# Second pass of a state-space layer: normalise before the last projection, with its weights held still

## The chip, the cores and the metric

The kernel runs on one core of one Trainium2 chip. The metric is device time in microseconds (us) of one execution, lower is better; the median of three runs is quoted. A core has these engines: PE (TensorE: matrix products and transposes from SBUF into PSUM, with weight loads shown apart as PEld), DVE (VectorE), ACT (ScalarE), POOL (GpSimd) and SP, which here issues the DMA transfers. Everything is in fp32, where one logical product is two PE instructions.

## The reference

The input x is 4 images of 64 channels and 256 x 256 pixels. Layer 0 adds a gated convolution with a spectral part to x; the change doesn't touch it. Layer 1 normalises its input by groups and runs two state-space blocks over the pixels, one along the rows (d = 0) and one along the columns (d = 1), and fuses them:

```
def s5_block(x, d):                  # x: tokens x 64 channels
    fx = layer_norm(x, ln1)          # over the channels
    h  = scan(fx)                    # forward and backward linear recurrence, + D * fx
    z  = gelu(h) + fx
    f2 = layer_norm(z, ln2)
    return f2 @ enc.T @ dec.T + f2
x = x + fusion_w @ concat(s5_block(rows, 0), s5_block(columns, 1)) + fusion_b
```

The part that matters is the last: the mean and variance of z over the 64 channels of each token, the scaling by 1 / sqrt(var + eps), and a 64 x 64 map per direction. The kernel folds the centring, the gain, enc, dec, the identity and the fusion into one matrix W of each direction (block `NB[d]` of the table `wb[d]`, the same 64 x 64 block twice on the diagonal). What is left at run time is the factor r = (var + eps)^-0.5 of each token, and the product with W.

## The kernel before, in words

Layer 0 leaves its result in `x1d` in DRAM. Layer 1 then goes over each of the 4 images in turn: pass A (`pass_a`) normalises, stores fx as `fxd` and sums up the states of short stretches; `scan` runs the recurrences over these summaries; pass B (`pass_b`), the one that is changed, works through the image again in 16 strips of 16 rows, each as two units: a column unit (d = 1), then a row unit (d = 0). So there are 32 units an image and 128 in all. The 128 partitions are 2 x 64 channels: their two halves are two sets of rows of the strip.

A unit holds 2048 columns of 128 partitions, in four blocks of 512, taken in the order `blocks = (1, 2, 0, 3)`. Its steps are:

- `load`: the unit's fx (1 MB) by one DMA, two units ahead, into one of three buffers.
- `states`: products of fx into the PSUM tile `pst` (one buffer of two banks), and for each half of it a DVE operation that advances the state (state x step + product), into `stm` or `sto`. A row unit does this in 8 parts of two steps, a column unit in 4 parts of one or two.
- `filt`: the products that make h of a block in PSUM (`ph`), then GELU on ACT, the addition of fx on POOL (together z, the tile `xr`), and the square `sq` on ACT.
- `sums`: products with a constant that give the sum of squares and the sum over 64 channels, for four blocks in one PSUM tile (`pv`), and a copy of it to SBUF on ACT.
- `rstd_of`: four transposes, four small DVE operations, and the power on POOL, so r lies with tokens on the partitions.
- `outputs`, for each block: four 128x128 products with z as the weights and W moving, which gives W z with tokens on the partitions (`px`), and one DVE multiplication with r (`y`).
- `emit`, for each block: four transposes of `y` back to channels on the partitions, and one DVE addition onto the strip's sum `acc`; for the row unit also the bias, and after the last block the four stores to the output.

The loop of pass B pipelines this over units. Iteration n has four quarters, i = 0 to 3, each of two parts. In quarter i it runs `filt` of unit n for one block, `states` of the next unit (in quarter 0 the last group of unit n itself), and late steps of units n - 1 and n - 2, by the table `behind`, whose key (4k + i, part) stands for the unit n - k. Before the change each quarter has an `outputs` and an `emit`; `sums` stands at (4, 1), `rstd_of` at (5, 1).

The order of instructions on PE and DVE is that of the program: products go through `mm`, DVE operations through the helper `vec`, and both are held in program order. ACT, POOL and SP instructions of pass B aren't held; the compiler places them by its own estimate of when they are ready. PSUM has eight banks: `pst` two, `ph` two, `pv` one, `px` three. In the profile, L1351 is `mm` of pass B, L303 the helper of DVE, L1469 the transposes in `rstd_of`, L1493 those in `emit`, L1445 GELU, L1446 POOL's addition, L1447 the square, L1460 the copy of the sums, L1476 the power, L1371 and L1377 the copies of carried states, L207 `mm` of layer 0.

Of the kernel before, what the change touches and what calls it, by code (L numbers as in the profile page):

```python
# [12 lines left out]
ALU = mybir.AluOpType  # L13
# [3 lines left out]
C = 64  # L17
HID = 170
S = 256
P = 128  # L20
# [8 lines left out]
NS0 = S // R0  # L29
R1 = 16  # L30
# [6 lines left out]
def _layout(parts):  # L37
# [8 lines left out]
    [("ident", 128), ("swap", 128), ("nswap", 128), ("cen", 128), ("gm", 128), ("on2", 34), ("sgn", 1), ("qf", 64),  # L46
# [12 lines left out]
def _constants():  # L59

    out = np.zeros((P, CONST_N), np.float64)

    def put(name, a):
        o, w = CONST_AT[name]
        out[: a.shape[0], o : o + w] = a

    eye = np.eye(P)
    swap = np.roll(eye, C, axis=0)
    put("ident", eye)
    put("swap", swap)  # L70
# [4 lines left out]
    put("on2", np.kron(np.eye(2, 34, 2), np.full((C, 1), 1.0 / C)))  # L75
    put("sgn", np.concatenate([-np.ones((C, 1)), np.ones((C, 1))]))
# [34 lines left out]
def tile_kernel(ctx: ExitStack, tc: tile.TileContext, x, cst, w0, winp, wdwp, w1, out):  # L111
    nc = tc.nc
# [17 lines left out]
    ident, swap, nswap = con("ident"), con("swap"), con("nswap")  # L130
# [63 lines left out]
    with ExitStack() as l0:  # L194
# [70 lines left out]
        stats1 = new(gpool, [P, 2 * NS0, 6], "stats0", 1)  # L265
# [12 lines left out]
        with ExitStack() as l1w:  # L278
            sp = l1w.enter_context(tc.tile_pool(name="prep1", bufs=1))
            lw = l1w.enter_context(tc.tile_pool(name="ldw", bufs=8))  # L280
# [796 lines left out]

    norms = new(gpool, [P, nb, 2], "norms", 1)
# [172 lines left out]
    def scan(tabs):  # L1251
        with ExitStack() as es:
# [8 lines left out]
            nc.vector.tensor_tensor(fold[:, 0], ident[:, 0:C], swap[:, 0:C], ALU.add)  # L1261
# [52 lines left out]
    def pass_b(b):  # L1314

        with ExitStack() as es:
# [6 lines left out]
            def load(s, d):  # L1323
                fx = new(ld, [P, 8 * S], "fx", 3)
                nc.sync.dma_start(out=fx, in_=fxd[b][s, d])
                return fx

            order = [(s, d) for s in range(NS1) for d in (1, 0)]
            units = []

            def unit(n):
                s, d = order[n]
                units.append({"s": s, "d": d, "fx": load(s, d)})

            nc.sync.dma_start(out=wb[1].rearrange("p a b -> p (a b)"), in_=wdb[1])
            unit(0)
            nc.sync.dma_start(out=wb[0].rearrange("p a b -> p (a b)"), in_=wdb[0])
            unit(1)
            accs = {0: load_strip(b, 0)}
# [17 lines left out]
            STEPS = (16, 8)  # L1357
# [21 lines left out]
            def states(u, i, part):  # L1379
# [5 lines left out]
                if d == 1:  # L1385
                    fx = u["fx"].rearrange("p (r w) -> p r w", r=8)
                    js = [j for j in (2 * i - 1, 2 * i) if j >= 0]
                    for n, j in enumerate(js):
                        mm(ps[:, n], lhsT=wb[1][:, j], rhs=fx[:, both(j, 7)], start=True, stop=True)
# [5 lines left out]
                fx = u["fx"].rearrange("p (q t) -> p q t", q=16)  # L1395
                js = (4 * i + 2 * part, 4 * i + 2 * part + 1)
                for n, j in enumerate(js):
                    for h in range(2):
                        p = slice(h * C, (h + 1) * C)
                        mm(  # L1400
                            ps[:, h, n * 256 : (n + 1) * 256], lhsT=wb[0][p, j], rhs=fx[p, both(j, 15)], start=True, stop=True
                        )
# [7 lines left out]
            def filt(u, i, part):  # L1410

                d, w = u["d"], wb[u["d"]]
                fx = u["fx"][:, i * 512 : (i + 1) * 512]
# [28 lines left out]
                xr, sq = new(wk, [P, 512], "xr", 8), new(wk, [P, 512], "sq", 4)  # L1442
# [7 lines left out]
            def sums(u):  # L1450

                ps = new(pp, [P, 512], "pv", 1)
                for k, name in enumerate(("sq", "xr")):
                    for i in range(4):
                        mm(
                            ps[32 * i : 32 * i + 32], lhsT=con("on2")[:, 2 - 2 * k : 34 - 2 * k], rhs=u[name, i], start=(k == 0),
                            stop=(k == 1),
                        )
                u["sums"] = new(wk, [P, 512], "sums", 1)
                nc.scalar.copy(u["sums"], ps)  # L1460
                for i in range(4):
                    u.pop(("sq", i))

            def rstd_of(u):

                ps = new(pp, [P, 512], "pv", 1)
                t = u.pop("sums")
                for k in range(4):
                    tc.keep_in_program_order(nc.tensor.transpose(ps[:, k * P : (k + 1) * P], t[:, k * P : (k + 1) * P], ident))  # L1469
                m = new(wk, [P, 16, 4], "m4")  # L1470
                vec.tensor_copy(m, ps.rearrange("p (n c) -> p n c", c=32)[:, :, 0:4])
                ve, r = new(wk, [P, 16, 2], "ve"), new(wk, [P, 32], "rs")
# [3 lines left out]
                nc.gpsimd.tensor_tensor(r, ve.rearrange("p n c -> p (n c)"), mhalf, ALU.pow)  # L1476
                u["r"] = r.rearrange("p (k i h) -> p k i h", k=4, i=4)

            def outputs(u, i):


                ps, xr = new(pp, [P, 512], "px", 3), u.pop(("xr", i))
                for k in range(4):
                    mm(ps[:, k * P : (k + 1) * P], lhsT=xr[:, k * P : (k + 1) * P], rhs=wb[u["d"]][:, NB[u["d"]]], start=True, stop=True)
                y = u["y", i] = new(wk, [P, 512], "y")
                yv, pv = (t.rearrange("p (k h c) -> p k h c", k=4, h=2) for t in (y, ps))
                vec.tensor_tensor(yv, pv, u["r"][:, :, i].unsqueeze(3).to_broadcast([P, 4, 2, C]), ALU.mult)

            def emit(u, i):
                y, acc = u.pop(("y", i)), u["acc"]  # L1490
                ps = new(pp, [P, 512], "px", 3)
                for k in range(4):
                    tc.keep_in_program_order(nc.tensor.transpose(ps[:, k * P : (k + 1) * P], y[:, k * P : (k + 1) * P], ident))  # L1493
                if u["d"] == 1:
                    o = acc[:, 2 * i : 2 * i + 2].rearrange("p r (g q) -> p r q g", q=16)
                    vec.tensor_tensor(o, ps.rearrange("p (r q g) -> p r q g", r=2, q=16), o, ALU.add)
                    return
                o = acc.rearrange("p r (g q) -> p q (r g)", q=16)[:, 4 * i : 4 * i + 4]
                vec.scalar_tensor_tensor(o, ps.rearrange("p (q t) -> p q t", q=4), bias, o, ALU.add, ALU.add)
                if i == blocks[-1]:  # L1500
                    for h, r, row in rows_of(u["s"]):
                        nc.sync.dma_start(out=out[b, :, row : row + 7 : 2, :], in_=acc[h, r])
# [4 lines left out]
            behind = {}  # L1507
            for i, k in enumerate(blocks):
                behind[7 + i, 1] = [(outputs, k)]
                behind[8 + i, 0] = [(emit, k)]  # L1510
            behind[4, 1] = [(sums,)]
            behind[5, 1] = [(rstd_of,)]

# [4 lines left out]
            for n in range(len(order) + 3):  # L1518
                if n < len(order):
                    s, d = order[n]  # L1520
                    units[n]["acc"] = accs[s]
                    if n + 2 < len(order):
                        unit(n + 2)
                    if d == 0 and s + 1 < NS1:
                        accs[s + 1] = load_strip(b, s + 1)
                    elif d == 0 and b + 1 < nb:
                        accs[NS1] = load_strip(b + 1, 0)
                for i in range(4):
                    m, group = (n, 3) if i == 0 else (n + 1, i - 1)

# [100 lines left out]
```

## Time and profile before

| | us |
|---|---|
| median of three runs (8789.25 to 8792.47) | 8791.17 |
| profiled execution: its span, first to last instruction (the profile gives no other time of it) | 8795.4 |
| PE busy in it | 8386.9 (95%) |
| DVE busy | 7055.1 (80%) |
| ACT busy | 3411.4 (39%) |
| POOL busy | 2401.9 (27%) |

The span of the profiled execution is 4.2 us above the median. A busy time is the union of an engine's instructions; matmuls are pipelined, so they overlap, and the distance between the starts of two steps says more than the length of one. Shapes are written as rows*columns of the weights, then the moving operand: `64*128 64x256` has weights of 64 rows and 128 columns, and 256 moving columns. A group of instructions is given with its count, busy time, mean duration in ns and the idle time before it with what ended that.

### The profile page before, as it was taken

How to read it: one execution, taken by the hardware profiler on the slowest of the kernel's cores; microseconds unless marked ns; L12 is line 12 of the kernel's file. 1: busy time of each engine (PE TensorE's matmuls, PEld its weight loads, DVE VectorE, ACT ScalarE, POOL GpSimd, SP SyncE). 2: the span in 40 equal slices, each digit the busy share in tenths (PEclk: the TensorE clock that was granted, in tenths of full speed). 3: DMA queues.
4: the chain of work that ended last, by engine and by line, in shares of the span. 5: the costliest groups of instructions: out<-in, count | busy, mean ns of one | idle time of the engine just before them, and what ended most of it. 6: DMA issues, size and time to landing. Idle time of an engine off the chain costs nothing. (4 is left out here: it accounts for less than half of the span.)

```text
span 8795.4 us, 184922 instructions
## 1 busy us (share of the span) xinstructions
PE 8386.9 (95%) x79478; PEld 5721.3 (65%) x79478; DVE 7055.1 (80%) x8837; ACT 3411.4 (39%) x5158; POOL 2401.9 (27%) x1282
## 2 busy tenths in 40 slices
PE   3999999999999999998999989999989999899999
PEld 2666666666666666665566657566655666565666
DVE  6999999999999999996767657776757677576766
ACT  3444444444444444445522237222264222462222
POOL 3000000000000000003734446544456444474444
PEclk9999999999999999999999999999999999999999
DMA  7444344444444333334423336133263233452332
GB/s 174 106 102 103 98 103 101 104 102 98 103 104 101 87 88 84 84 80 142 151 68 82 91 90 214 59 80 89 73 183 116 80 82 80 123 196 53 82 89 65
DMA packets 655264, 904.19 MB, mean 103 GB/s; under 512 B 43120, under 2 KB 584816, under 8 KB 618864
## 3 DMA queue, kind: packets, MB, share of 16 engines
q1 hardware_dynamic: 654448, 892.37, 37.9%
q8 instruction: 627, 10.27, 0.5%
q14 instruction: 189, 1.55, 0.1%
HBM read 583.86 MB, written 275.05 MB: 98 GB/s over the span
## 5 line engine op out<-in xcount | busy, mean ns | idle before, releaser
L207 PE MATMUL m<-v,sw 64*128 64x256 f32 (+1 forms) x8192 | 1542.8, 393 | 1.5 <-DVE v L303 1.1
L207 PEld LDWEIGHTS m<-v,sw 64*128 64x128 f32 (+1 forms) x8192 | 1123.4, 188 | 504.0 <-issue 359.0
L303 DVE SCALAR_TENSOR_TENSOR acc<-xat,taps,acc 128x1024 f32<-128x1024 f32 x1024 | 1311.0, 1280 | 16.6 <-ACT acc L164 2.9
L1446 POOL TENSOR_TENSOR xr<-xr,fx 128x512 f32<-128x512 f32 x512 | 650.3, 1270 | 1862.3 <-ACT xr L1445 1367.7
L1351 PE MATMUL pst<-fx,wb 64*128 64x256 f32 (+1 forms) x4992 | 1016.1, 438 | 37.5 <-DVE stm L303 18.3
L694 POOL MEMSET at<- 64x256 f32 x4 | 1.2, 308 | 3526.2 <-DVE v L303 3526.2
L1351 PEld LDWEIGHTS pst<-fx,wb 64*128 64x128 f32 (+1 forms) x4992 | 508.8, 187 | 370.4 <-issue 244.1
L1476 POOL TENSOR_TENSOR rs<-ve,mhalf 128x32 f32<-128x32 f32 x128 | 695.3, 5432 | 99.5 <-DVE ve L303 99.5
L303 DVE SCALAR_TENSOR_TENSOR stm<-stm,step,pst 128x512 f32<-128x512 f32 x640 | 478.5, 748 | 232.9 <-PE pst L1351 219.4
L1447 ACT ACTIVATE sq<-xr 128x512 f32<-128x512 f32 x512 | 322.9, 631 | 873.7 <-POOL xr L1446 873.7
L207 PEld LDWEIGHTS m<-ct,hw 128*64 128x64 f32 x16384 | 509.8, 138 | 117.6 <-issue 117.6
L303 DVE SCALAR_TENSOR_TENSOR sto<-sto,step,pst 128x512 f32<-128x512 f32 x512 | 382.9, 748 | 242.4 <-PE pst L1351 231.1
L1351 PE MATMUL px<-wb,xr 128*128 128x128 f32 x4096 | 574.1, 284 | 0.0
L1351 PEld LDWEIGHTS px<-wb,xr 128*128 128x128 f32 x4096 | 524.2, 194 | 54.0 <-issue 41.8
L303 DVE TENSOR_TENSOR y<-px,rs 128x512 f32<-128x512 f32 x512 | 354.0, 691 | 230.6 <-PE px L1351 221.6
L1351 PE MATMUL ph<-sto,wb 128*64 128x128 f32 (+1 forms) x5120 | 528.1, 299 | 0.0
L207 PE MATMUL m<-ct,hw 128*64 128x64 f32 x16384 | 527.4, 223 | 0.0
L1351 PE MATMUL ph<-stm,wb 128*64 128x128 f32 (+1 forms) x5120 | 525.1, 299 | 0.0
L1351 PEld LDWEIGHTS ph<-stm,wb 128*64 128x64 f32 (+1 forms) x5120 | 409.3, 147 | 144.2 <-issue 127.9
L1351 PEld LDWEIGHTS ph<-sto,wb 128*64 128x64 f32 (+1 forms) x5120 | 405.3, 147 | 142.7 <-issue 129.6
L1445 ACT ACTIVATE xr<-ph 128x512 f32<-128x512 f32 x256 | 152.8, 597 | 825.9 <-PE ph L1351 825.9
L164 POOL TENSOR_TENSOR rs<-ve,mhalf 128x32 f32<-128x32 f32 x64 | 347.6, 5432 | 398.5 <-DVE ve L303 386.8
(317 smaller groups left out, 15636.0 us busy)
## 6 DMA issues: line engine op xcount, KB each, us to landing
strip<-x1d SPq DMA_DIRECT2D x512, 256.0 KB, 7.3
fx<-fxd SPq DMA_DIRECT2D x128, 1024.0 KB, 6.9
at<-in_x_dram SPq DMA_DIRECT2D x248, 320.0 KB, 4.6
sx<-in_x_dram SPq DMA_DIRECT2D x256, 256.0 KB, 4.0
pr<-in_x_dram SPq DMA_DIRECT2D x256, 256.0 KB, 4.1
er<-in_x_dram SPq DMA_DIRECT2D x256, 256.0 KB, 4.0
x1d<-x SPq DMA_DIRECT2D x256, 256.0 KB, 3.9
fxd<-fv SPq DMA_DIRECT2D x64, 1024.0 KB, 4.7
```

The source lines that it names most:

```text
L164: return lambda *args, **kw: tc.keep_in_program_order(getattr(self.engine, name)(*args, **kw))
L207: tc.keep_in_program_order(nc.tensor.matmul(*args, **kw))
L303: tc.keep_in_program_order(getattr(nc.vector, name)(*args, **kw))
L694: nc.gpsimd.memset(at[C:P, 4, 1 : S + 1], 0.0)
L1351: tc.keep_in_program_order(nc.tensor.matmul(*args, **kw))
L1445: nc.scalar.activation(xr, ps if d == 1 else xr, AF.Gelu_apprx_tanh)
L1446: nc.gpsimd.tensor_tensor(xr, xr, fx, ALU.add)
L1447: nc.scalar.activation(sq, xr, AF.Square)
L1476: nc.gpsimd.tensor_tensor(r, ve.rearrange("p n c -> p (n c)"), mhalf, ALU.pow)
```

## The change

The order of the last two operations is turned round: z is multiplied by r first, with channels on the partitions, and then projected with W as the weights and z moving, so the result comes out with channels on the partitions.

- `rstd_of` writes the power into a tile `wide`, cleared once per image, at two of each 32 columns.
- `rows_back` (new): four transposes of `wide`, and an ACT copy into `rows`: the factors of block i lie as rows 32i and 32i + 1.
- `scale` (new), twice per unit, for a pair of blocks: two products of 32 rows, with the constant `pick` as weights, spread the factors over the 64 channels of each half in two banks of PSUM; one DVE multiplication of 128x1024 scales z in place.
- `project` (new), twice per unit: four products with 64x64 weights (one block of W each), 512 moving columns, into two banks; then one DVE addition of 128x1024 onto the sum. The products read z in the order of the output, so the moving operand steps by 16 elements (column unit) or 128 elements (row unit).
- `outputs` and `emit` are gone. The table of late steps becomes: `sums` (4, 1), `rstd_of` (5, 1), `rows_back` (7, 1), `scale` (8, 0) and (8, 1), `project` (9, 0) and (9, 1). The stores come with the second `project` of a row unit.
- The strip's sum lies differently on the partitions (`load_sum`, `rows_at`): halves by the upper and lower eight rows.
- fx is loaded in two halves, outer blocks (0, 3) and inner blocks (1, 2), the inner one in quarter 2 and into two buffers; z is kept in pairs of blocks.
- PSUM: `pst` two banks, `ph` two, and a tile `two` of two banks, twice, for all late steps. Constant `swap` is gone and `pick` added; `stats1` moves to another pool; some buffers go from two to one.

```diff
-            def load(s, d):
-                fx = new(ld, [P, 8 * S], "fx", 3)
-                nc.sync.dma_start(out=fx, in_=fxd[b][s, d])
-                return fx
+            def load(u, inner):
+                t = u["fx", inner] = new(ld, [P, 1024], f"fx{inner}", 2 if inner else 3)
+                v = fxd[b][u["s"], u["d"]]
+                if inner:
+                    nc.sync.dma_start(out=t, in_=v[:, 512:1536])
+                else:
+                    nc.sync.dma_start(
+                        out=t.rearrange("p (k c) -> p k c", k=2),
+                        in_=v.rearrange("p (k c) -> p k c", k=4)[:, 0:4:3],
+                    )
...
-                nc.gpsimd.tensor_tensor(r, ve.rearrange("p n c -> p (n c)"), mhalf, ALU.pow)
-                u["r"] = r.rearrange("p (k i h) -> p k i h", k=4, i=4)
-
-            def outputs(u, i):
-                ps, xr = new(pp, [P, 512], "px", 3), u.pop(("xr", i))
-                for k in range(4):
-                    mm(ps[:, k * P : (k + 1) * P], lhsT=xr[:, k * P : (k + 1) * P], rhs=wb[u["d"]][:, NB[u["d"]]], start=True, stop=True)
-                y = u["y", i] = new(wk, [P, 512], "y")
-                yv, pv = (t.rearrange("p (k h c) -> p k h c", k=4, h=2) for t in (y, ps))
-                vec.tensor_tensor(yv, pv, u["r"][:, :, i].unsqueeze(3).to_broadcast([P, 4, 2, C]), ALU.mult)
-
-            def emit(u, i):
...
+                nc.gpsimd.tensor_tensor(
+                    wide.rearrange("p k (i c) -> p (k i) c", c=32)[:, :, 0:2], ve,
+                    mhalf.rearrange("p (n c) -> p n c", c=2), ALU.pow,
+                )
+
+            def rows_back(u):
+                ps = new(pp, [P, 2, 512], "two")[:, 0]
+                turn_blocks(ps, lambda k: wide[:, k])
+                u["rows"] = new(wk, [P, 512], "rows", 1)
+                nc.scalar.copy(u["rows"], ps)
+
+            def scale(u, n):
+                k = u["first"][n]
+                ps, x = new(pp, [P, 2, 512], "two"), u["pairs"][k]
+                for place, i in enumerate((k, 2 + k) if u["d"] == 1 else (2 * k, 2 * k + 1)):
+                    p = slice(32 * i, 32 * i + 32)
+                    mm(ps[:, place], lhsT=con("pick")[p], rhs=u["rows"][p], start=True, stop=True)
+                vec.tensor_tensor(x, x, ps, ALU.mult)
+
+            def project(u, n):
+                d, k = u["d"], u["first"][n]
+                x, ps = u["pairs"].pop(k), new(pp, [P, 2, 512], "two")
+                for hi in range(2):
+                    for h in range(2):
+                        p = slice(h * C, (h + 1) * C)
+                        if d == 1:
+                            v = x[p, hi].rearrange("p (r q g) -> p r g q", r=2, q=16)
+                        else:
+                            v = x[p].rearrange("p b (q r g) -> p r g (b q)", q=4, r=8)[:, 4 * hi : 4 * hi + 4]
+                        mm(ps[hi * C : (hi + 1) * C, h], lhsT=wb[d][p, NB[d], p], rhs=v, start=True, stop=True)
+                if d == 1:
+                    o = u["acc"][:, :, 2 * k : 2 * k + 2].rearrange("p k r w -> p k (r w)")
+                    vec.tensor_tensor(o, ps, o, ALU.add)
+                    return
+                o = u["acc"].rearrange("p k r (g q) -> p (k r) g q", q=16)[:, :, :, 8 * k : 8 * k + 8]
+                vec.scalar_tensor_tensor(
+                    o, ps.rearrange("p k (r g q) -> p (k r) g q", r=4, g=16), bias, o, ALU.add, ALU.add
+                )
...
             blocks = (1, 2, 0, 3)
-            behind = {}
-            for i, k in enumerate(blocks):
-                behind[7 + i, 1] = [(outputs, k)]
-                behind[8 + i, 0] = [(emit, k)]
-            behind[4, 1] = [(sums,)]
-            behind[5, 1] = [(rstd_of,)]
+            behind = {
+                (4, 1): [(sums,)], (5, 1): [(rstd_of,)], (7, 1): [(rows_back,)], (8, 0): [(scale, 0)],
+                (8, 1): [(scale, 1)], (9, 0): [(project, 0)], (9, 1): [(project, 1)],
+            }
...
+                    if i == 2 and n + 2 < len(order):
+                        load(units[n + 2], True)
```

More of the change, by code (lines that the diff above doesn't have):

```diff
@@ L45 @@
 CONST_AT, CONST_N = _layout(
-    [("ident", 128), ("swap", 128), ("nswap", 128), ("cen", 128), ("gm", 128), ("on2", 34), ("sgn", 1), ("qf", 64),
+    [("ident", 128), ("nswap", 128), ("cen", 128), ("gm", 128), ("on2", 34), ("pick", 128), ("sgn", 1), ("qf", 64),
      ("qi2", 128), ("qj", 128), ("selt", 128)]
@@ L69, in _constants @@
     put("ident", eye)
-    put("swap", swap)
     put("nswap", -swap)
@@ L75, in _constants @@
     put("on2", np.kron(np.eye(2, 34, 2), np.full((C, 1), 1.0 / C)))
+    put("pick", np.kron(np.ones((4, 1)), np.kron(np.eye(32, 2), np.ones((1, C)))))
     put("sgn", np.concatenate([-np.ones((C, 1)), np.ones((C, 1))]))
@@ L128, in con @@
         return ct[:, o : o + w] if o < CONST_0 else tables[0][:, o - CONST_0 : o - CONST_0 + w]
-    ident, swap, nswap = con("ident"), con("swap"), con("nswap")
+    ident, nswap = con("ident"), con("nswap")
     mhalf = new(cpool, [P, 32], "mhalf")
@@ L264, in tile_kernel @@
         fxd = [new(dpool, [NS1, 2, P, 8 * S], f"fxd{b}") for b in range(nb)]
-        stats1 = new(gpool, [P, 2 * NS0, 6], "stats0", 1)
         prm = new(cpool, [P, 2, 9], "prm")
@@ L279, in tile_kernel @@
             sp = l1w.enter_context(tc.tile_pool(name="prep1", bufs=1))
+            stats1 = new(sp, [P, 2 * NS0, 6], "stats0", 1)
             lw = l1w.enter_context(tc.tile_pool(name="ldw", bufs=8))
@@ L1075, in load_strip, with rows_at, load_sum @@
         return t
+    def rows_at(s, k, hi):
+        row = s * R1 + 8 * hi + (k ^ hi)
+        return slice(hi * C, (hi + 1) * C), slice(row, row + 7, 2)
+    def load_sum(b, s):
+        t = new(ring, [P, 2, 4, S], "strip")
+        for k in range(2):
+            for hi in range(2):
+                half, rows = rows_at(s, k, hi)
+                nc.sync.dma_start(out=t[half, k], in_=x1d[b][:, rows, :])
+        return t
     norms = new(gpool, [P, nb, 2], "norms", 1)
@@ L1260, in scan @@
             fold = new(wp, [P, 3, C], "fold")
-            nc.vector.tensor_tensor(fold[:, 0], ident[:, 0:C], swap[:, 0:C], ALU.add)
+            nc.vector.tensor_tensor(fold[:, 0], ident[:, 0:C], nswap[:, 0:C], ALU.subtract)
             nc.vector.tensor_tensor(fold[:, 1], ident[:, 0:C], nswap[:, 0:C], ALU.add)
@@ L1321, in pass_b, with block_of, mirrored_pair @@
             wb = [new(wp, [P, NB[d] + 1, P], f"wb{d}") for d in range(2)]
-            def load(s, d):
-                fx = new(ld, [P, 8 * S], "fx", 3)
-                nc.sync.dma_start(out=fx, in_=fxd[b][s, d])
-                return fx
+            def load(u, inner):
[8 more added lines that the diff above has]
+                    )
+            def block_of(u, i):
+                o = 512 * (i // 2)
+                return u["fx", i in (1, 2)][:, o : o + 512]
+            def mirrored_pair(u, j):
+                n = STEPS[u["d"]]
+                inner = n // 4 <= j < 3 * n // 4
+                t = u["fx", inner].rearrange("p (q t) -> p q t", q=n // 2)
+                return t, both(j - n // 4 if inner else j if j < n // 4 else j - n // 2, n // 2 - 1)
+            STEPS = (16, 8)
             order = [(s, d) for s in range(NS1) for d in (1, 0)]
@@ L1332, in unit @@
                 s, d = order[n]
-                units.append({"s": s, "d": d, "fx": load(s, d)})
+                units.append({"s": s, "d": d})
+                load(units[n], False)
             nc.sync.dma_start(out=wb[1].rearrange("p a b -> p (a b)"), in_=wdb[1])
             unit(0)
+            load(units[0], True)
             nc.sync.dma_start(out=wb[0].rearrange("p a b -> p (a b)"), in_=wdb[0])
             unit(1)
-            accs = {0: load_strip(b, 0)}
+            load(units[1], True)
+            accs = {0: load_sum(b, 0)}
             scan(tabs)
@@ L1351, in mm @@
                 tc.keep_in_program_order(nc.tensor.matmul(*args, **kw))
-            STEPS = (16, 8)
+            wide = new(wk, [P, 4, P], "wide", 1)
+            nc.gpsimd.memset(wide, 0.0)
             def step_of(u, j):
@@ L1385, in states @@
                 if d == 1:
-                    fx = u["fx"].rearrange("p (r w) -> p r w", r=8)
                     js = [j for j in (2 * i - 1, 2 * i) if j >= 0]
                     for n, j in enumerate(js):
-                        mm(ps[:, n], lhsT=wb[1][:, j], rhs=fx[:, both(j, 7)], start=True, stop=True)
+                        fx, pair = mirrored_pair(u, j)
+                        mm(ps[:, n], lhsT=wb[1][:, j], rhs=fx[:, pair], start=True, stop=True)
                     for n, j in enumerate(js):
@@ L1394, in states @@
                     return
-                fx = u["fx"].rearrange("p (q t) -> p q t", q=16)
                 js = (4 * i + 2 * part, 4 * i + 2 * part + 1)
                 for n, j in enumerate(js):
+                    fx, pair = mirrored_pair(u, j)
                     for h in range(2):
@@ L1400, in states @@
                         mm(
-                            ps[:, h, n * 256 : (n + 1) * 256], lhsT=wb[0][p, j], rhs=fx[p, both(j, 15)], start=True, stop=True
+                            ps[:, h, n * 256 : (n + 1) * 256], lhsT=wb[0][p, j], rhs=fx[p, pair], start=True, stop=True
                         )
@@ L1412, in filt @@
                 d, w = u["d"], wb[u["d"]]
-                fx = u["fx"][:, i * 512 : (i + 1) * 512]
+                fx = block_of(u, i)
                 if d == 1:
@@ L1441, in filt @@
                 ps = u.pop("ph")
-                xr, sq = new(wk, [P, 512], "xr", 8), new(wk, [P, 512], "sq", 4)
+                k, place = (i % 2, i // 2) if d == 1 else (i // 2, i % 2)
+                if k not in u["pairs"]:
+                    u["pairs"][k] = new(wk, [P, 2, 512], "xr", 6)
+                xr, sq = u["pairs"][k][:, place], new(wk, [P, 512], "sq", 4)
                 if d == 0:
@@ L1450, in sums @@
             def sums(u):
-                ps = new(pp, [P, 512], "pv", 1)
+                ps = new(pp, [P, 2, 512], "two")[:, 0]
                 for k, name in enumerate(("sq", "xr")):
@@ L1455, in sums, with turn_blocks @@
                         mm(
-                            ps[32 * i : 32 * i + 32], lhsT=con("on2")[:, 2 - 2 * k : 34 - 2 * k], rhs=u[name, i], start=(k == 0),
-                            stop=(k == 1),
+                            ps[32 * i : 32 * i + 32], lhsT=con("on2")[:, 2 - 2 * k : 34 - 2 * k], rhs=u.pop((name, i)),
+                            start=(k == 0), stop=(k == 1),
                         )
-                u["sums"] = new(wk, [P, 512], "sums", 1)
+                u["sums"] = new(wk, [P, 512], "rows", 1)
                 nc.scalar.copy(u["sums"], ps)
-                for i in range(4):
-                    u.pop(("sq", i))
+            def turn_blocks(ps, v):
+                for k in range(4):
+                    tc.keep_in_program_order(nc.tensor.transpose(ps[:, k * P : (k + 1) * P], v(k), ident))
             def rstd_of(u):
-                ps = new(pp, [P, 512], "pv", 1)
-                t = u.pop("sums")
-                for k in range(4):
-                    tc.keep_in_program_order(nc.tensor.transpose(ps[:, k * P : (k + 1) * P], t[:, k * P : (k + 1) * P], ident))
-                m = new(wk, [P, 16, 4], "m4")
+                ps, t = new(pp, [P, 2, 512], "two")[:, 0], u.pop("sums")
+                turn_blocks(ps, lambda k: t[:, k * P : (k + 1) * P])
+                m = new(wk, [P, 16, 4], "m4", 1)
                 vec.tensor_copy(m, ps.rearrange("p (n c) -> p n c", c=32)[:, :, 0:4])
-                ve, r = new(wk, [P, 16, 2], "ve"), new(wk, [P, 32], "rs")
+                ve = new(wk, [P, 16, 2], "ve", 1)
                 vec.scalar_tensor_tensor(ve, m[:, :, 2:4], -1.0, m[:, :, 2:4], ALU.mult, ALU.mult)
@@ L1475, in rstd_of @@
                 vec.tensor_scalar(ve, ve, 0.0, LN_EPS, ALU.max, ALU.add)
-                nc.gpsimd.tensor_tensor(r, ve.rearrange("p n c -> p (n c)"), mhalf, ALU.pow)
-                u["r"] = r.rearrange("p (k i h) -> p k i h", k=4, i=4)
-            def outputs(u, i):
-                ps, xr = new(pp, [P, 512], "px", 3), u.pop(("xr", i))
-                for k in range(4):
-                    mm(ps[:, k * P : (k + 1) * P], lhsT=xr[:, k * P : (k + 1) * P], rhs=wb[u["d"]][:, NB[u["d"]]], start=True, stop=True)
-                y = u["y", i] = new(wk, [P, 512], "y")
-                yv, pv = (t.rearrange("p (k h c) -> p k h c", k=4, h=2) for t in (y, ps))
-                vec.tensor_tensor(yv, pv, u["r"][:, :, i].unsqueeze(3).to_broadcast([P, 4, 2, C]), ALU.mult)
@@ L1489, in emit @@
-            def emit(u, i):
[L1490 to L1496, printed above, removed]
-                    return
[L1498 to L1502, printed above, removed]
@@ L1506, in pass_b @@
-            blocks = (1, 2, 0, 3)
-            behind = {}
-            for i, k in enumerate(blocks):
-                behind[7 + i, 1] = [(outputs, k)]
-                behind[8 + i, 0] = [(emit, k)]
-            behind[4, 1] = [(sums,)]
-            behind[5, 1] = [(rstd_of,)]
+                nc.gpsimd.tensor_tensor(
[3 more added lines that the diff above has]
+            def rows_back(u):
+                ps = new(pp, [P, 2, 512], "two")[:, 0]
+                turn_blocks(ps, lambda k: wide[:, k])
+                u["rows"] = new(wk, [P, 512], "rows", 1)
+                nc.scalar.copy(u["rows"], ps)
@@ new lines, in scale @@
+            def scale(u, n):
[8 more added lines that the diff above has]
+                x, ps = u["pairs"].pop(k), new(pp, [P, 2, 512], "two")
+                for hi in range(2):
+                    for h in range(2):
[8 more added lines that the diff above has]
+                    vec.tensor_tensor(o, ps, o, ALU.add)
+                    return
+                o = u["acc"].rearrange("p k r (g q) -> p (k r) g q", q=16)[:, :, :, 8 * k : 8 * k + 8]
+                vec.scalar_tensor_tensor(
+                    o, ps.rearrange("p k (r g q) -> p (k r) g q", r=4, g=16), bias, o, ALU.add, ALU.add
+                )
+                if n == 1:
+                    for k in range(2):
+                        for hi in range(2):
+                            half, rows = rows_at(u["s"], k, hi)
+                            nc.sync.dma_start(out=out[b, :, rows, :], in_=u["acc"][half, k])
@@ L1520, in pass_b @@
                     s, d = order[n]
-                    units[n]["acc"] = accs[s]
+                    units[n]["acc"], units[n]["pairs"] = accs[s], {}
+                    units[n]["first"] = (1, 0) if d == 1 else (0, 1)
                     if n + 2 < len(order):
@@ L1524, in pass_b @@
                     if d == 0 and s + 1 < NS1:
-                        accs[s + 1] = load_strip(b, s + 1)
+                        accs[s + 1] = load_sum(b, s + 1)
                     elif d == 0 and b + 1 < nb:
```

## The prediction, made before the changed kernel was run

> **What bounds the kernel now.** I read the page first, for which engine fills the span and where. Its share line, and rows "PE" and "PEclk" of its 40 slices (busy tenths, and granted TensorE clock in tenths):
>
> ```profile
> PE 8386.9 (95%) x79478; PEld 5721.3 (65%) x79478; DVE 7055.1 (80%) x8837; ACT 3411.4 (39%) x5158; POOL 2401.9 (27%) x1282
> PE   3999999999999999998999989999989999899999
> PEclk9999999999999999999999999999999999999999
> ```
>
> TensorE is busy in every slice at nearly its full clock. The chain of waits names almost only PE steps in the second pass and comes back to the same ten-instruction ph step every 50.19 us (8013.75, 8063.94, 8114.12): one strip, that is one column unit and one row unit. 64 strips take 3212 of the span's 8795.4 us. So I price the change in that stage, as PE time per strip.
>
> Second view: the timeline of PE there (start, length from first start to last end). The useful number is the distance from one start to the next, since ends overlap. Two quarters of a column iteration with row-unit states, then one of a row iteration:
>
> ```profile
> 8282.18 1.05 PE L1351 MATMUL px<-wb,xr 128*128 128x128 f32 x8
> 8283.17 1.14 PE L1351 MATMUL pst<-fx,wb 64*128 64x256 f32 x8
> 8284.23 0.66 PE L1493 MATMUL px<-ct,y 128*128 128x128 f32 x4
> 8284.73 1.02 PE L1351 MATMUL ph<-fx,wb 128*128 128x512 f32 x2
> 8285.59 1.03 PE L1351 MATMUL ph<-sto,wb 128*128 128x256 f32 x4
> 8286.54 1.13 PE L1351 MATMUL pst<-fx,wb 64*128 64x256 f32 x8
> 8287.61 1.13 PE L1351 MATMUL ph<-sto,wb 128*128 128x256 f32 x4
> ...
> 8256.23 1.16 PE L1351 MATMUL px<-wb,xr 128*128 128x128 f32 x8
> 8257.23 1.88 PE L1351 MATMUL pst<-fx,wb 128*128 128x512 f32 x4
> 8258.95 0.60 PE L1493 MATMUL px<-ct,y 128*128 128x128 f32 x4
> 8259.48 1.97 PE L1351 MATMUL ph<-sto,wb 128*64 128x128 f32 x32
> ```
>
> Steps stand end to end: `outputs` 0.99, `emit` 0.50 to 0.53, row states 1.06, column states 1.72, column filter 1.82 + 0.97, row filter 1.90. A logical fp32 product is two instructions, 0.43 us each per 512 columns (ph<-fx: 0.86 for two). PE waits for almost nothing: what it is given is the time.
>
> Third view: groups by form in 8000 to 8702.6 us, fourteen strips (busy, mean ns | idle before):
>
> ```profile
> L303 DVE TENSOR_TENSOR y<-px,rs 128x512 f32<-128x512 f32 x110 | 76.1, 692 | 49.6 <-PE px L1351 49.6
> L303 DVE TENSOR_TENSOR strip<-px,strip 128x512 f32<-128x512 f32 x56 | 57.3, 1023 | 0.0
> L1460 ACT COPY sums<-pv 128x512 f32<-128x512 f32 x29 | 16.7, 576 | 1.9
> L1371 ACT COPY sto<-sf 128x256 f32<-128x256 f32 x14 | 8.8, 631 | 0.0
> L1377 ACT COPY cy<-sf 128x128 f32<-128x128 f32 x28 | 7.0, 296 | 17.0 <-DVE sto L303 17.0
> ```
>
> These show what a strided operand costs. The strip addition steps through SBUF by 64 bytes and takes 1.02 us against 0.69 for y. The sums and cy copies fix ScalarE at 0.73 ns an element plus 0.20; sto<-sf steps by 1 KB and takes (0.631 - 0.204)/256 = 1.67 ns.
>
> Last, layer 0 and one more group, for shapes the change brings:
>
> ```profile
> 2006.33 1.09 PE L207 MATMUL two<-en,w0t 64*64 64x512 f32 x8
> 2011.52 1.07 PE L207 MATMUL two<-en,ga 64*128 64x512 f32 x4
> 2002.41 1.75 PE L207 MATMUL m<-v,sw 128*128 128x256 f32 x7
> ...
> 8265.39 1.89 PE L1351 MATMUL ph<-stm,wb 128*128 128x256 f32 x8
> ```
>
> The first is exactly `project`'s shape with contiguous moving data: four tiles at once, 0.91 us to the next step. The second is two row tiles at once: 0.92 to 1.00. The last two are the same shape, moving data at 8-byte steps (v14) and contiguous: (1.75 - 0.39)/6 = 0.227 against (1.89 - 0.38)/7 = 0.216 us. Stepping already costs 5%.
>
> **The change part by part, per strip.** Removed from PE: 8 `outputs` x 0.99 and 8 `emit` transposes x 0.51, 12.0 us.
>
> Added: 2 `rows_back` x 0.53 (four transposes, as sums' own) = 1.06. 4 `scale` at 0.96, by the second row above (two row tiles, two banks; 32 rows instead of 64 is bounded by one at a time, 1.8, and I stay with the row) = 3.84. 4 `project`, the disputed term.
>
> `project` moves its columns by 16 elements (64 bytes, column unit) or 128 (512 bytes, row unit). No PE row shows more than 8 bytes. Lower end: the contiguous row, 0.91. Near upper end: at 8 bytes two columns share 16 bytes and 256 columns take 0.227 us, 1.77 ns for each 16 bytes; if that is a limit, a lone column costs 1.77 ns, near ScalarE's 1.67. Then 2 x 512 x 1.77 = 1.82, + 0.10 for changing tile shape = 1.92. Far end: the two column tiles on the same 64 partitions share one such limit, 3.73; against it, sums' 128*32 products stream four different operands at full rate (eight instructions in 1.06 us). I take 1.92, because three engines agree: 4 x 1.92 = 7.68. Three shape changes where neighbours had none: 0.30. Added 12.9; the stream grows by 0.9.
>
> [...]
>
> Waits, which `outputs` and `emit` covered. `pst` has one buffer: row states, two DVE updates of 0.75, and only then the next row states. The shortest distance in the trace is 8239.37 to 8242.23, 2.86 us. In quarters 2 and 3 of a column iteration nothing is left between them. From the second states of quarter 2 to the next: 1.06 + 0.97 = 2.03, a stall of 0.83. The same after quarter 3 with `rows_back` between: 2.53, a stall of 0.33. In quarter 1 `rstd_of`'s four small DVE operations (0.21, 0.32, 0.19, 0.18) now queue behind a 1.22 us addition that starts 0.28 before the following row states; they end some 1.9 us after that start, where DVE is due at 1.18 (8269.95 to 8271.13): about 0.6. In a row iteration `rows_back` needs the power: sums' transposes at 8251.65, power's end at 8259.65, 8.0 us; PE now arrives after 0.53 and two quarters of 1.72 + 0.10 + 1.90, 7.97, and DVE's addition stands before the chain: about 0.5. Queued behind that wait are the next states, and so everything. Sum 2.3. Ends: 1.0 (only the first and some of the rest) to 3.3 (`scale` waiting another 0.5 per unit for the rows copy).
>
> Off the path. DVE: 8 x 0.69 + 4 x 1.02 + 4 x 1.11 = 14.1 becomes 6 x 1.22 (hw<-two,wsp, 128x1020) + 2 x 1.28 (acc<-xat) = 9.9; it had about 15 us of slack, worth nothing. ACT: one copy more per unit, 0.58, behind the GELU; ready about 1.5 us after the filter, PE reaches `scale` after 1.9 to 2.3. POOL: same power, 5.43 us, other layout; one memset per image. SP: fx in two halves, 128 issues more, landing after some 7 us and used 20 later; the inner one waits for POOL's add and holds back the next outer half, strip load and stores, none due within a quarter; stores leave two quarters earlier. PSUM stays at eight banks, and each `two` buffer is free two steps before its next use. The constants' moves cost nothing that a row shows. Each pass's end: from the last power to the last addition 12.1 us before, 9.6 by the same rows after; with overlap, -5 in all.
>
> Sum: 64 x (0.9 + 2.3) - 5 = +200 us: 8995 on the profiled execution's span of 8795.4, the one time it has, which stands 4.2 above the 8791.17 median; on the median **8990**. With the ends of the waits, and `project` 0.05 lower or 0.10 higher: 64 x (0.7 + 1.0) to 64 x (1.3 + 3.3), 8900 to 9085.
>
> **The rivals.**
> - *Strided reading is free.* `project` costs 0.91: 64 x (0.9 - 4.04 + 2.3) - 5 = -59, 8732; with the waits at 1.0, 8650. For: contiguous data at this shape runs so, and PE, DVE and ACT need not share a limit. Against: the 5% at 8 bytes. The point is a `project` step of 1.13 us; below it the change gains.
> - *The rows copy stands behind the last Square on ACT.* ACT's order isn't pinned. GELU, POOL's add (1.27) and Square (0.63) then end before it: `scale` waits 2.0 us in each of 128 units, less the stalls it takes in, +235: 9225. Against: carry copies in the trace stand where they are ready.
> - *The two column tiles share one limit:* 64 x 7.24 more, 9450.
> - *It doesn't do what it says:* weights would be reloaded with each product, as the equal counts of PE and PEld suggest. They load beside the stream, so no time hangs on it.
>
> **How the numbers follow.** Forecast 0.71; free reading 0.19; copy behind Square 0.06; shared limit 0.02; nothing measurable 0.02. A measurement of this kernel can tell 0.2%, 18 us, from no change. Faster 0.20: free reading, and a little of the forecast's low tail. Same 0.04: prices near 1.13. Slower 0.76. The range reaches into the free-reading case to its middle and past the forecast's high end: 8725 to 9100. The forecast's own: 8900 to 9085.
>
> **What would show it.** PE and PEld at 76918 each: per unit 48 instructions go and 28 come. `project`'s eight instructions in groups about 0.9 us apart and 1.9 us in all; 0.43 and 0.91 would prove me wrong, and the sign with it. `scale` 0.96. Strip period near 53.4 us. Row states 2.86 apart in quarters 2 and 3, with PE released by DVE; `rows_back` released by POOL. Square before the rows copy would mean the second rival.

## The result and the profile after

The changed kernel takes **9073.17 us** (median of four runs, 9072.04 to 9074.44) against 8791.32 in the runs beside it: 1.0319 times the time before, interval 1.0305 to 1.0334, or 282 us more. The forecast was 8990, its range 8725 to 9100. The profiled execution has a span of 9070.4, 275 above the one before.

The page of the changed kernel, the rows that answer to those of before:

```profile
PE 8567.4 (94%) x76918; PEld 5177.3 (57%) x76918; DVE 6782.6 (75%) x8325; ACT 3471.7 (38%) x5286; POOL 2406.0 (27%) x1286
PE   3999999999999999989999989999899999899998
PEclk9999999999999999999999999999999999899999
```

PE has 2560 instructions fewer, exactly as worked out, and is busy 180 us longer. The mean granted clock is 0.985 against 0.988, and steps whose neighbours stay the same keep their length (products of `sq` in `sums`, 0.88 us from start to next start in both), so the clock isn't what costs. The fewer instructions are slower ones.

The timeline of PE in the second pass (start, length; in brackets the idle time before, and what ended it): a row unit's two `project` steps and what follows each, a column unit's second one, and then quarters 2 and 3 of a column iteration:

```profile
8476.55 2.23 PE L1388 MATMUL two<-xr,wb 64*64 64x512 f32 x8
8478.72 1.97 PE L1388 MATMUL ph<-stm,wb 128*64 128x128 f32 x32
8480.61 2.35 PE L1388 MATMUL two<-xr,wb 64*64 64x512 f32 x8
8482.89 0.66 PE L1505 MATMUL two<-ct,rows 128*128 128x128 f32 x4
...
8506.93 2.13 PE L1388 MATMUL two<-xr,wb 64*64 64x512 f32 x8
8509.00 0.66 PE L1505 MATMUL two<-ct,rows 128*128 128x128 f32 x4
...
8512.80 1.13 PE L1388 MATMUL pst<-fxTrue,wb 64*128 64x256 f32 x8 [0.17 <-DVE stm L303]
8513.87 1.13 PE L1388 MATMUL ph<-sto,wb 128*128 128x256 f32 x4
8515.65 1.13 PE L1388 MATMUL pst<-fxTrue,wb 64*128 64x256 f32 x8 [0.66 <-DVE stm L303]
```

Three things are to be seen. From start to next start `project` takes 2.17 and 2.28 us in the row unit and 2.07 in the column unit (its first one 1.86). The two row states are 2.85 us apart, with PE idle for 0.66 until DVE has advanced the state: the recurrence that the prediction named. And this is small beside `project`.

In the group by form (8310.67 to 8961.47 us; busy, mean ns of one, idle before) `project` has waited for nothing:

```profile
L1388 PE MATMUL two<-xr,wb 64*64 64x512 f32 x384 | 104.6, 1146 | 0.0
```

Adding the distances from start to next start over the second pass gives the account per strip, in us. Gone: `outputs` and `emit`, 12.01. Added: `project` 8.44, `scale` 4.23, `rows_back` 1.0, and 1.0 on steps that stood there before and now have neighbours of another tile shape (column states +0.48, fx products of `filt` +0.41, transposes of `rstd_of` +0.11, the column filter +0.18, the row filter -0.18); waits 1.4 (0.83 and 0.33 for the two recurrence stalls, 0.23 ahead of the row states in quarter 2), of which the profile marks 1.06 as idle time. Net +4.04, and 64 x 4.04 = 259 of the span's 275. Cutting the trace at the sums' products says the same in another way: 264 within the four second passes (the next image's first pass included), 7 between the last sums of a first pass and the first of the second, 3 after the last sums, 1 ahead of layer 1's first sums.

### The profile page after: what moved, and what is told of

Its sections match the earlier page's. It is cut to its first block, busy times and chain, and to the rows that moved or that the text cites. A ratio compares the mean times of both kernels' runs of the same rounds, so it can differ in the third digit from the quotient of the medians.

```text
span 9070.4 us, 180041 instructions
## 1 busy us (share of the span) xinstructions
PE 8567.4 (94%) x76918; PEld 5177.3 (57%) x76918; DVE 6782.6 (75%) x8325; ACT 3471.7 (38%) x5286; POOL 2406.0 (27%) x1286
## 5 line engine op out<-in xcount | busy, mean ns | idle before, releaser
L1517 POOL TENSOR_TENSOR wide<-ve,mhalf 128x32 f32<-128x32 f32 x128 | 695.6, 5435 | 296.1 <-DVE ve L303 197.5
L1487 POOL TENSOR_TENSOR xr<-xr,fxTrue 128x512 f32<-128x512 f32 x256 | 327.2, 1278 | 1534.4 <-ACT xr L1486 1534.4
L1388 PE MATMUL pst<-fxTrue,wb 64*128 64x256 f32 (+1 forms) x2560 | 548.6, 441 | 67.7 <-DVE stm L303 65.2
L1388 PE MATMUL two<-xr,wb 64*64 64x512 f32 x2048 | 554.9, 1144 | 5.5 <-DVE xr L303 5.5
L1388 PE MATMUL pst<-fxFalse,wb 64*128 64x256 f32 (+1 forms) x2432 | 493.7, 434 | 25.9 <-DVE stm L303 16.3
L303 DVE TENSOR_TENSOR xr<-xr,two 128x1024 f32<-128x1024 f32 x256 | 311.0, 1217 | 203.5 <-PE two L1388 203.5
L303 DVE TENSOR_TENSOR hw<-two,wsp 128x1020 f32<-128x1020 f32 (+1 forms) x384 | 421.1, 1097 | 42.7 <-PE two L207 32.1
L164 POOL TENSOR_TENSOR rs<-ve,mhalf 128x32 f32<-128x32 f32 x64 | 347.7, 5432 | 395.2 <-DVE ve L303 390.6
```

The costliest lines, as they stand in the source:

```text
L164: return lambda *args, **kw: tc.keep_in_program_order(getattr(self.engine, name)(*args, **kw))
L303: tc.keep_in_program_order(getattr(nc.vector, name)(*args, **kw))
L1388: tc.keep_in_program_order(nc.tensor.matmul(*args, **kw))
L1487: nc.gpsimd.tensor_tensor(xr, xr, fx, ALU.add)
L1517: nc.gpsimd.tensor_tensor(wide.rearrange("p k (i c) -> p (k i) c", c=32)[:, :, 0:2], ve, mhalf.rearrange("p (n c) -> p n c", c=2), ALU.pow,)
```

## The experiments

**Theory 1.** `project` is slow because of the step of its moving operand: from 16 bytes on a column costs some 1.7 ns. This is the author's estimate, from 0.227 us for 256 columns at 8 bytes (1.77 ns for two of them) and ScalarE's 1.67 ns an element at a step of 1 KB; the expectations below put it as one fetch per column, which no trace shows. **Rival.** The order of the steps is what costs: the recurrence stalls, or a copy that comes late.

**e1: `project` reads contiguous data.** In e1, e2, e3 and e5 the result is in another order of pixels than the reference's.

```diff
-   v = x[p, hi].rearrange("p (r q g) -> p r g q", r=2, q=16)
+   v = x[p, hi]
...
-   v = x[p].rearrange("p b (q r g) -> p r g (b q)", q=4, r=8)[:, 4 * hi : 4 * hi + 4]
+   v = x[p, hi]
```

> The changed kernel with project reading its moving columns contiguously; what it leaves out is the reordering, so pixels land in the wrong places. First theory (the price is the step of the moving operand): the step of project falls from the 1.86 to 2.28 us seen in the changed kernel to 0.96, 4 x 0.96 = 3.8 instead of 8.4 us per strip, 64 x 4.6 = 294 us less than 9073, about 8780. Second theory (the price is the waits and the changes of tile shape that the new order of late steps brings): project gets shorter but the waits take it back; 9000 or more. A project step above 1.5 us would refute the first.

Measured: 8805.2 us, 1.0013 times before (1.0003 to 1.0022), where about 8780 was expected; `project` takes 1.02 us from start to next start. Its group, 8200 to 8700 us:

```profile
L1388 PE MATMUL two<-xr,wb 64*64 64x512 f32 x320 | 43.6, 615 | 0.0
```

615 ns for one against 1146, and 268 us of the 282 are gone: the stride is the cause. The other half of the reading is as useful. With the stride free, the change still gains nothing. Its steady strips do gain: 49.92 us from the sums of one to the sums of the next against 50.19, 17 us in 64 strips. The first and last units of each second pass (0.85 and 2.95 us longer between sums) and 8 us between the first passes and the second take it back.

**e2 and e3: other steps.** The same lines with `"p (n k) -> p k n"`, and k elements from one column to the next.

```diff
+   v = x[p, hi].rearrange("p (n k) -> p k n", k=...)   # k in e2: column unit 2, row unit 4; in e3: 8 and 16
```

> The changed kernel with other steps of project's moving operand, which puts pixels in the wrong places: 8 bytes in column units, 16 bytes in row units. If a fetch serves 16 bytes and takes 1.67 to 1.77 ns: column units 0.96 to 1.0 us per project, row units 1.85 to 1.95; about 8910 us. If the price needs a long step (64 bytes and more): both near 0.96, about 8780. If the price grows with each byte of step: row units in between, 1.2 to 1.4.

> The changed kernel with steps of 32 bytes in column units and 64 in row units (pixels land wrong). If one fetch per column is the whole price: both 1.86 to 1.96 us per project, so row units lose their excess (2.17 and 2.28 at 512 bytes) and the time is about 9035. If row units are dearer for another reason than their step (other engines at work at that time): they stay at 2.2 and the time at 9065 or more. If the price grows with the step: column units at 1.4 to 1.6.

Measured: 8921.56 and 9037.55 us (one run each), both near the theory. The timeline of PE in e2, row unit (16 bytes) and then column unit (8 bytes):

```profile
8403.54 2.01 PE L1388 MATMUL two<-xr,wb 64*64 64x512 f32 x8
8405.47 1.97 PE L1388 MATMUL ph<-stm,wb 128*64 128x128 f32 x32
...
8427.45 1.13 PE L1388 MATMUL two<-xr,wb 64*64 64x512 f32 x8
8428.51 1.12 PE L1388 MATMUL ph<-fxTrue,wb 128*128 128x512 f32 x2
```

From start to next start, medians:

| step of the moving operand | bytes | `project`, us |
|---|---|---|
| contiguous (e1) | 4 | 1.02 |
| e2, column unit | 8 | 1.06 |
| e2, row unit | 16 | 1.94 |
| e3, column unit | 32 | 1.97 |
| e3, row unit | 64 | 1.99 (1.86 to 2.03) |
| the change, column unit | 64 | 1.86 for the first, 2.06 for the second |
| the change, row unit | 512 | 2.25 (2.16 to 2.28) |

Nearly all of the price comes between 8 and 16 bytes: 1.06 against 1.94 us, and 1.94 is 1.9 times the contiguous 1.02. The runs show these times and not what lies behind them; no run had a step between 8 and 16. At 64 bytes the row unit loses its excess (1.99 against 2.25 us), so this is due to the step of 512 bytes and not to what else runs at that time. Why one step of 64 bytes takes 1.86 in one place and 2.06 in another no run shows.

**e4: spread the steps.** `scale` and `project` of the second pair move one to two quarters back, into the quarters where PE waits for the recurrence.

```diff
-   (8, 1): [(scale, 1)], (9, 0): [(project, 0)], (9, 1): [(project, 1)],
+   (9, 0): [(scale, 1)], (10, 1): [(project, 0)], (11, 1): [(project, 1)],
```

> The changed kernel with its late steps spread: the second scale in (9, 0), project in (10, 1) and (11, 1), so that quarters 2 and 3 have work between two row-unit states again. First theory (the waits are an own term beside the step of the operand, 1.3 us per strip in the trace of the changed kernel: 0.73 + 0.33 + 0.23): they go but for some 0.3 that comes up in quarter 1; 64 x 1.0 = 64 us less, about 9010. Second theory (waits are the larger part): 8900 or less. If PE's waits were hidden by something else: within 20 us of 9073.

Measured: 8998.19 us, 1.0233 (1.0216 to 1.0250), 75 less than the change. PE's waits for DVE's recurrence, the change in 8310 to 8961 us and then e4 in 8200 to 8700 us (us in total, times, longest):

```profile
PE pst L1388 <- DVE stm L303: 12.7, 36, 0.7
...
PE pst L1388 <- DVE stm L303: 3.4, 9, 0.4
```

The stalls were real and could be filled. But they are not the whole 75: a steady strip is 0.78 us shorter, 50 us in 64, of which PE's idle time is 0.50 and `project`, 8.23 instead of 8.44 us, is 0.21; most of the other 25 us lies in the first and last units of the passes. So the forecast of 9010 came near partly by luck, and the stalls are a smaller part of the loss than the 75 of 282 us.

**e5 and e7: both at once; e6: the reorder moved to DVE.** e5 is e1 with e4's table. e6 has the reference's order again: the multiplication in `scale`, on DVE, writes its result reordered into a new tile `xs`, and `project` reads that contiguously; z has four pair buffers instead of six. e7 is e6 with e4's table.

```diff
-   vec.tensor_tensor(x, x, ps, ALU.mult)
+   xs = u["scaled"][k] = new(wk, [P, 2, 512], "xs", 2)
...
+   if u["d"] == 1:
+       o, x, ps = o.rearrange("p (r g q) -> p r q g", r=4, g=16), *(t.rearrange("p (r q g) -> p r q g", r=4, q=16) for t in (x, ps))
...
+   vec.tensor_tensor(o, x, ps, ALU.mult)
```

> Contiguous moving data and spread late steps together (the reordering is left out, so pixels land in the wrong places). If the two are separate terms, the 75 us that spreading took from the changed kernel come off the contiguous one too: 8805 - 75 = 8730, 0.993 of the kernel before. If shorter project steps no longer cover quarters 2 and 3 (they put 1.02 us where 0.83 and 0.33 are missing, so they should), or the power on POOL now ends last: 8770 or more.

> The reordering moved from project's moving operand to the output of scale's multiplication on DVE, which then steps by 64 or 32 bytes in its writes; the whole computation is there. If DVE is off the path: time as in the contiguous kernel, 8805, within 15 us, with the multiplication at about 1.9 us instead of 1.22 (the 128x512 addition with a 64-byte step took 1.02 against 0.69). If the longer multiplication delays the state updates behind it on DVE by as much as it grows, 4 x 0.7 us per strip: up to 8805 + 64 x 2.8 = 8985.

> The same with the late steps spread, a whole computation and a candidate to beat both kernels. Stepped operand and waits both gone: 8730 to 8760, 0.993 to 0.996 of the kernel before. If only one of them can be had, 8790 or more: no gain over the kernel before.

Measured: e5 8844.25 us (1.0060, 1.0045 to 1.0075), e6 8813.73 (1.0025, 1.0015 to 1.0036), e7 8866.05 (1.0085, 1.0070 to 1.0101). e6 is what was expected: its DVE group shows what the reorder costs there, 1973 ns instead of 1217, and the time stays within 9 us of e1's. This multiplication is not on the path.

```profile
L303 DVE TENSOR_TENSOR xs<-xr,two 128x1024 f32<-128x1024 f32 x40 | 78.9, 1973 | 16.1 <-PE two L1388 16.1
```

e5 and e7 are misses: filling the stalls made both slower, by 39 us against e1 and 52 against e6. The view of PE's waits, 8200 to 8700 us of e7 (us in total, times, longest), shows why; the first line was not there in e6, and e5 has it with 12.9 us:

```profile
PE two L1388 <- ACT rows L1527: 16.1, 20, 1.1
PE pst L1388 <- DVE stm L303: 3.8, 10, 0.4
```

and in the timeline of e7:

```profile
8427.60 0.63 ACT L1488 ACTIVATE sq<-xr 128x512 f32<-128x512 f32 x1 [1.38 <-POOL xr L1487]
8428.13 0.57 ACT L1527 COPY rows<-two 128x512 f32<-128x512 f32 x1
...
8428.75 1.13 PE L1388 MATMUL two<-rows,ct 32*128 32x512 f32 x4 [1.10 <-ACT rows L1527]
```

`scale` waits for the copy of the factors, and the copy stands behind the last Square, which waits for POOL. This is the second rival of the prediction. In the change itself the copy comes first (8521.36, the Square at 8522.84), so there it costs nothing. In e7's program a `project` of the unit before comes ahead of `rows_back` in the same part of quarter 3, so the four transposes of `rows_back` come later. That this is why the compiler placed the copy after the Square is tried next.

**e10: e7 with `rows_back` ahead of `project`.**

```diff
-   for k in (2, 1, 0):
+   for k in (1, 2, 0):
```

> As e7, with one change in the order written for TensorE: in a chunk slot where both halves of a strip have steps, rows_back of the one half stands ahead of project of the other. Theory (in e7 ScalarE's rows copy came behind the Square because rows_back's transposes stood behind project in TensorE's order, and scale waited 1.4 us per strip for it): the copy comes ahead of the Square again, 64 x 1.4 = 90 us less, about 8775 us against e7's 8866. Rival (the copy's place on ScalarE is set by something else): it stays within 15 us of 8866.

Measured: 8766.25 us, 0.9970 (0.9959 to 0.9982), 100 less than e7. ACT in e10 in the corresponding quarter, and the `scale` of PE:

```profile
8533.69 0.57 ACT L1527 COPY rows<-two 128x512 f32<-128x512 f32 x1
8536.17 0.63 ACT L1488 ACTIVATE sq<-xr 128x512 f32<-128x512 f32 x1 [1.38 <-POOL xr L1487]
```

```profile
8535.86 1.13 PE L1388 MATMUL two<-rows,ct 32*128 32x512 f32 x4
```

The copy comes 2.5 us ahead of the Square, `scale` has no idle time before it, and the time is near the 8775 expected. The theory holds and the rival (ACT's order set by something else) falls.

**e9: e6 with a table that meets both conditions:** a `project` fills a quarter in which PE waited, and nothing stands ahead of `rows_back` in its part of the quarter.

```diff
-   (8, 1): [(scale, 1)], (9, 0): [(project, 0)], (9, 1): [(project, 1)],
+   (8, 1): [(scale, 1)], (9, 1): [(project, 0)], (10, 1): [(project, 1)],
```

> As e6, with the steps of the row half spread otherwise: its sums stand in the fourth chunk slot, its rstd in the fifth, its rows_back in the seventh, then scale and the four products of project for the column half and for the row half in slots 8 to 10, so that rows_back follows the filter at once and the second quarter of the column iteration has products to fill its recurrence. Theory of the stalls (a product waits about 0.73 us per strip on VectorE's recurrence in that quarter, because nothing else is queued there): e6's 1.30 us of stalls per strip fall to about 0.56, 64 x 0.74 = 47 us, so about 8766 us from e6's 8813.7, 0.997 of the kernel before. Rival (the stall only moves, to the quarter that gave its products away): 8800 us or more.

Measured: 8758.05 us, 0.9958 (0.9944 to 0.9971), where 8766 was expected. The recurrence's is still PE's only wait; 8200 to 8700 us of e6, then of e9:

```profile
PE pst L1388 <- DVE stm L303: 10.7, 30, 0.7
...
PE pst L1388 <- DVE stm L303: 4.3, 21, 0.2
```

This version beats both kernels: 35 us under the one before, 315 under the change. A steady strip takes 49.14 us against 50.19 before, 67 us in 64 strips; about half of that is lost again where passes start and end.

**e8: the kernel before with fx loaded in halves** and nothing else of the change.

```diff
-   fx = new(ld, [P, 8 * S], "fx", 3)
-   nc.sync.dma_start(out=fx, in_=fxd[b][s, d])
+   t = u["fx", inner] = new(ld, [P, 1024], f"fx{inner}", 2 if inner else 3)   # two DMAs, the inner one in quarter 2
...
```

> The kernel before with one part of the change alone: fx loaded in an outer and an inner half, the inner one in quarter 2. By the working of the prediction it costs nothing: within 10 us of the kernel before. If the added issues hold back the stores and strip loads on SP: some 0.5 us per unit or more, 8855 or more.

Measured: 8800.48 us, 1.0010 (1.0000 to 1.0020), 8 us more. The distance from the last sums of a first pass to the first of the second grows by 8.0 us over the four images in the profiled executions (from 165.7 to 170.3 us each, to 167.9 to 170.7), and the strip's median period stays at 50.19. So it is a cost of starting a pass, as far as one execution of each shows, and none within it.

## Why the prediction was right, and where its sizes were off

It was right in the sign and the mechanism, and 83 us low. Of the forecast's +200, 64 x 3.2 = 205 were in the strips; measured there are 259. (Its own range, 8900 to 9085, is counted on the span and so stands 4 us too high for the median.) By its own steps:

- **`project` 7.68: measured 8.44.** The column unit is as priced: 1.86 and 2.06 against 1.92, with 0.88 us from one pass of 512 columns to the next, 0.97 for some: 1.72 ns a column, or 1.9, where 1.77 was taken. The row unit, at 512 bytes, takes 1.04 to 1.09 us a pass. What is mis-sized is "a lone column costs 1.77 ns", as one price for both: it fits 16 to 64 bytes (1.86 to 2.06 us a `project`), and at 512 bytes a column costs 2.0 to 2.1 ns. Why isn't settled; no run had a step between 64 and 512. The 1.77 rests on the assumption that two columns at 8 bytes share one such price, which no row of before shows; e2 measured 1.06 us at 8 bytes and 1.94 at 16.
- **`scale` 3.84: measured 4.23.** 1.057 each, not the row's 0.96. Its group was the nearest row and still 10% low.
- **Shape changes 0.30: measured 1.0,** the largest miss in proportion. It counted three changes inside the added steps; the account shows longer steps before and after them as well. The 0.10 us for each is the author's estimate; how much of the 1.0 is the change of shape alone was not tried by itself.
- **`rows_back` 1.06: measured 1.0.**
- **Waits 2.3: measured 1.4.** The two recurrence stalls are there as priced, 0.83 and 0.33 (2.85 us between row states whose two steps take 2.02). The chain of `rstd_of` gives 0.23 instead of 0.6, and the power's 0.5 is absent. The reason shows in the row unit's chain, before and after:

```profile
8252.32 1.26 POOL L1446 TENSOR_TENSOR xr<-xr,fx 128x512 f32<-128x512 f32 x1 [4.65 <-issue]
8252.71 0.92 DVE L303 SCALAR_TENSOR_TENSOR ve<-m 128x32 f32<-128x32 f32 x1
8254.22 5.43 POOL L1476 TENSOR_TENSOR rs<-ve,mhalf 128x32 f32<-128x32 f32 x1 [0.64 <-DVE ve L303]
...
8484.53 0.19 DVE L303 SCALAR_TENSOR_TENSOR ve<-m 128x32 f32<-128x32 f32 x1
8485.34 5.43 POOL L1517 TENSOR_TENSOR wide<-ve,mhalf 128x32 f32<-128x32 f32 x1 [1.80 <-PE pst L1388]
```

  DVE's addition does stand before the chain, but `ve` takes 0.19 us instead of 0.92. Before, it began while POOL's addition ran and ended 0.05 us after it; in the change none of the 128 begins while that addition runs. So the power ends 7.88 us after the transposes of the sums began (8482.89 to 8490.77) instead of 8.0, and PE, which comes after 8.02, does not wait. The prediction had taken over the 0.92 with the 8.0.
- **Ends of passes -5: measured +11.** Between the first passes and the second the change lost 7 us and e8, with the split loads alone, 8, where the forecast had put nothing: it looked at the steady state, in which the loads are hidden. The 5 us that the forecast gained at the ends don't show.
- **Off the path: right.** In e6 each multiplication on DVE takes 0.76 us more, 3 us a strip, and the time stays within 9 us of e1's.

The sum: too little by 0.76 + 0.39 + 0.7 a strip, too much by 0.9 of waits and 0.06 of `rows_back`; 0.89 x 64 = 57, and 16 at the ends, make 73 of the 83. That waits too dear made up for steps too cheap is luck; without it the forecast would have been about 58 us lower still.

The rivals. *Strided reading is free* falls with the table of steps, and the chance of 0.19 paid for a real doubt: no row of before showed more than 8 bytes. Its price was wrong, though. e1 is this case, made by hand: 8805, not 8732; and the point of 1.13 us at which `project` would turn the sign is too high for the whole kernel, since at 1.02 the change is not yet a gain. What it left out is what the forecast left out: dearer `scale`, dearer neighbours and starts. *The rows copy behind the last Square* did not decide the change, and decided e5 and e7; there it made `scale` wait 0.8 us on average in e7 and 1.1 at most, where the prediction had put 2.0. *The shared limit* falls: `project` takes 1.9 to 2.3, not 3.73.

## What to carry to other kernels

Price a moving operand by its step in bytes: in these fp32 products 8 bytes were nearly free (1.06 us against 1.02 contiguous), and 16 about doubled the time (1.94); if another engine touches the data anyway and is off the path, let that engine write it in the order that the product wants (on DVE 1973 ns instead of 1217, and e6 within 9 us of e1). When steps of another tile shape come in, price the neighbours too (1.0 us a strip here), and look at where a stage starts (7 us here), not only at its steady state. When steps are moved to fill a stall, check what the move delays: here the same filling cost 52 us (e7 against e6) or gained 47 (e10 against e6), by the place of four transposes.

## What the runs showed of the hardware that was not expected

- The price of a stride is a step, not a slope, up to 64 bytes: 1.06 us at 8 bytes, 1.94 at 16, 1.86 to 2.06 at 64; and at 512 it is higher again, 2.16 to 2.28.
- Four 64x64 products at once, two of them on the same 64 partitions, pay this price once and not twice: 1.97 us for the eight instructions at 32 bytes against 1.02 contiguous, where the prediction's estimate for a shared limit was 3.73.
- DVE's multiplication with reordered writing (steps of 64 or 32 bytes) takes 1973 ns against 1217, 1.6 times, for 128x1024 elements.
- A small DVE operation that begins while POOL's 128x512 addition runs ends with it: in the kernel before, the 120 instances of `ve` from `m` that began so ended 0.04 to 0.05 us after that addition, after up to 1.2 us, where 8 others took 0.2 us. Why they end together was not tried.
